# Gate and up: S3·T3 of four units in seven products, with kept parts read back by SyncE's queue

## The chip, the cores and the metric

The kernel runs on one core of a Trainium2 chip, in one launch. The metric is the device time of one execution in microseconds (us); a version's time is the median of its runs. The engines of a core run side by side, each through its own list of instructions, and wait for each other by semaphores: PE (TensorE, matmuls out of SBUF into the accumulators of PSUM), DVE (VectorE), ACT (ScalarE), POOL (GpSimd) and SP (SyncE, which here only starts DMAs). DMAs are started from SP, ACT and POOL; those that add onto their destination are started from POOL.

## The reference

All numbers are fp32; x is 2 x 2048 x 512. What is computed:

```python
x = x + attn(layernorm(x), Wq, Wk, Wv, Wo)      # softmax over 512 x 512 scores, per batch
n = layernorm(x)
gate = einsum('bsh,oh->bso', n, lut[gate_idx])  # 1376 rows; lut has 16 entries
up   = einsum('bsh,oh->bso', n, lut[up_idx])
out  = x + einsum('bsh,oh->bso', silu(gate) * up, lut[down_idx])
```

The change lies in `gate` and `up` and the product `silu(gate) * up`. The attention in front and the product with `down_idx` behind are the same in both kernels but for one choice of accumulators.

## The kernel before

**The stages.** By the clock of the profiled execution: Gram products of the normalised input to 78 us, squares and products of the attention's matrices to 180, the attention's output (y) to 286, gate and up to 748, the last 96 rows of gate and up to 789, the product down to the end.

**Gate and up.** The 1376 hidden rows are eleven blocks f of 128 (the last has 96), the 4096 tokens eight chunks of 512, taken in pairs p = 0..3. A unit (f, p) computes gate and up of block f for the two chunks of pair p. Eight units with f = 0 and 1 come first, then 32 units (f, p), f = 2..9, p = 0..3, in order; the eleventh block goes through `LastRows`. Block rows "gate, up" and the two halves of the contracted 512 make a 2 x 2 block matrix A, the two chunks and the two halves another, B. One level of Strassen's method in Winograd's form computes their product with seven block products instead of eight, with sums S1..S4 of A's blocks and T1..T4 of B's:

- a1 `11·11` gives p1; a2 adds `S2·T2` onto it in the same accumulator, giving u2; a3 adds `S1·T1`; a4 adds `S4·22`;
- c1 `S3·T3` gives p7; c2 adds `22·T4`;
- b adds `12·21` onto p1 and makes h0, the gate of the first chunk.

From these come h0 = silu(p1 + 12·21), times u2 + c; and h1 = silu(a after a4), times c22 = (a after a3) + p7. Each of the seven is two matmul calls of 128 x 512 (one per 128 rows of the contracted 256). A call is two matmul instructions in the profile, at line 1065 (`mm`).

**The second level.** Three of the seven products are themselves done for four units at once, by `Second` (line 946): `of_b` does `12·21`, `of_c` does `22·T4`, `of_d` does `S4·22`. The four units are two blocks f (even and odd) by two pairs p. The two calls of each unit are again a 2 x 2 product of blocks, eight calls, done as seven. Their left factors (of the weights) are summed per pair of f by `sums_left` (four sums on DVE), their right factors (of the tokens) once per group g = p // 2 by `sums`, in f = 1 and 2. These right factors T1, T2, T4 are written to DRAM (`far`) and read back when needed by `load`, on ACT's DMA queue, into tiles of tag "tt" (TT of them).

**Roles.** With f > 1 a unit has role 2·(f mod 2) + p mod 2: role 0 is the even f's first unit of the group, 1 its second, 2 the odd f's first, 3 its second. Role 1 also computes two products that belong to roles 2 and 3. They are copied out of PSUM by ACT (`part`, tiles of tag "rt", RT of them) and kept in DRAM as r6 (for role 2) and r5 (for role 3). Role 2 computes one more product and adds it onto r5 there, by POOL (`onto`). Roles 2 and 3 get their kept part back: `add_part` adds it onto p1 (of_b) and u2 (of_c) by a DMA of POOL, and `back` loads it as a tile y (of_d), also by POOL. With this, p=0 and p=1 are group 0, p=2 and p=3 group 1.

**Order.** The order of instructions on PE, ACT, DVE and SP is written out by hand in `Line.run`. The unit before (`last`) is finished within the unit that runs: its `first` (the product for h0 and its store, on SP), its `a4`, `end` (silu of h1) and `out` (the product for h1 and its store). At each `between` one due load, one entry of `todo`, and as many sums and steps of the weights' lookup as keep DVE within a lead (`leads[0]`, in us) of PE by a count of their costs are put in. The lookup makes the weights of later blocks from their indices on DVE (TENSOR_SCALAR at line 330, COPY_PREDICATED at line 342); after it come the four sums of a block (line 379). The helper `add` on DVE is line 172, `evict`, a copy on ACT, line 181; h1 and h0 are stored by SP at line 1092. DVE, ACT and PE each work through their list in order, so an instruction that waits holds all that stands behind it on its engine; the same is true of the DMA issues on SP and POOL.

**Accumulators.** PSUM has eight banks of 128 x 512: tag "a" has two, "c" two, and "b", "x", "z", "w" (of_b, of_c, of_d) one each. `Down` uses "a", "b" and "c".

Of the kernel before, what the change touches and what calls it, by code (L numbers as in the profile page):

```python
# [62 lines left out]
P = 128  # L63
# [6 lines left out]
def tile_attn_ffn(  # L70
# [874 lines left out]
    def psum(tag, name):  # L945
        return fps.tile([P, E], F32, tag=tag, name=name, bufs=2 if tag in "ac" else 1)

    class Second:
# [8 lines left out]
        def sums(self, g):  # L957
# [4 lines left out]
            def made(tag, u, v):  # L962
                r[tag] = x2p.tile([P, CH], F32, tag="tt", name=f"{tag}_{self.name}{g}", bufs=TT)
                sub(r[tag], u(), v())
                far = self.far[g, tag] = dram.tile(
                    [P, CH], F32, tag=f"{self.name}{g}{tag}", name=f"far_{self.name}{g}{tag}"
                )
                nc.gpsimd.dma_start(far, r[tag])
# [12 lines left out]
        def ready(self, f):  # L981
            return f in gu if self is of_d else f in uw
# [45 lines left out]
        def back(self, u):  # L1028

            t = u.temp("y")  # L1030
            nc.gpsimd.dma_start(t, self.parts[u.p // 2, {2: "r6", 3: "r5"}[u.role]])
            return t

    RT, TT = 3, 8
# [7 lines left out]
    seconds = [of_c, of_b, of_d]  # L1042
# [6 lines left out]
    def loads(f, p):  # L1049

        g = p // 2
        if 1 < f < NFT - 1 and f % 2 == 0 and p % 2:
            order = [(of_c, "T2"), (of_c, "T1")]
            order += [(o, tag) for tag in ("T2", "T1") for o in (of_d, of_b)]
        elif 1 < f < NFT - 1 and f % 2 and p % 2 == 0:
            order = [(o, "T4") for o in seconds]
        else:
            order = []
        return [lambda o=o, tag=tag: o.load(g, tag) for o, tag in order]
# [11 lines left out]
    class GateUp:  # L1071
# [32 lines left out]
        def extra0(self):  # L1104
            if self.role == 1:
                of_c.go_on(self, "S2", "T2")
                of_c.part(self, "r6")
            elif self.role == 2:
                of_c.begin(self, "S3", "T3")
                of_c.part(self, "r5", onto=True)  # L1110

        def c1(self):
            self.c = self.view("c")
            mm(self.c, self.pairs("S3", "T3"), True)
            self.p7 = self.temp("p7")
            evict(self.p7, self.c)
# [7 lines left out]
        def c2(self):  # L1124
            if self.role is None:
                mm(self.c, self.pairs("22", "T4"), False)
                add(self.u2, self.c, self.u2)
            elif self.role == 0:
# [3 lines left out]
                add(self.u2, self.c, self.u2)  # L1132
            elif self.role == 1:
                add(self.u2, self.c, self.u2)
                of_c.go_on(self, "S4", "22")
                add(self.u2, of_c.ps, self.u2)
            elif self.role == 2:
                of_c.go_on(self, "22", "T4")

        def extra1(self):  # L1140
            if self.role == 1:
                of_c.go_on(self, "S1", "T1")
                of_c.part(self, "r5")
            elif self.role == 2:
                of_b.begin(self, "S3", "T3")
                of_b.part(self, "r5", onto=True)

        def extra2(self):
            if self.role == 1:
                of_d.go_on(self, "S2", "T2")  # L1150
                of_d.part(self, "r6")
                of_b.go_on(self, "S2", "T2")
                of_b.part(self, "r6")

        def extra3(self):
            if self.role == 1:
                of_d.go_on(self, "S1", "T1")
                of_d.part(self, "r5")
                of_b.go_on(self, "S1", "T1")
                of_b.part(self, "r5")  # L1160
            elif self.role == 2:
                of_d.begin(self, "S3", "T3")
                of_d.part(self, "r5", onto=True)
            if self.role in (2, 3):
                self.y = of_d.back(self)

        def b(self):
# [14 lines left out]
            if self.role != 1:  # L1182
                nc.scalar.activation(h0, self.p1 if self.role in (None, 3) else h0, AF.Silu)

        def silu(self):

            if self.role == 1:
                nc.scalar.activation(self.h0, self.h0, AF.Silu)

        def a3(self):  # L1190
            mm(self.a, self.pairs("S1", "T1"), False)
            self.c22 = self.temp("c22")
            add(self.c22, self.a, self.p7)

        def first(self):
            if self.role == 2:
                add(self.u2, of_c.ps, self.u2)
            if self.role in (2, 3):
                add(self.u2, self.c, self.u2)
# [3 lines left out]
        def kept(self):  # L1203
            add(self.y, of_d.ps, self.y)

        def a4(self):
            self.h1 = h1 = self.temp("h1")
# [11 lines left out]
            else:  # L1219
                if self.role == 2:  # L1220
                    mm(self.a, of_d.pair(self, "22", "T4"), False)
                add(h1, self.a, self.y)
# [10 lines left out]
    class Line:  # L1233
# [5 lines left out]
        def run(self, u, final=False):  # L1239
            last, self.last = self.last, u  # L1240

            role = getattr(u, "role", None)
            u.a1()
            if last is not None:
                last.silu()
            self.between()
            before = getattr(last, "role", None)
            if before == 1:
                last.first()
            u.extra0()  # L1250
            u.c1()
            self.between()
            if before == 2:
                last.kept()
            elif before == 3:
                last.first()
            u.extra1()
            if role != 3 and last is not None:
                last.a4()
                self.between()  # L1260
            u.a2()
            if role == 3:
                self.between(0.0)
                last.a4()
                last.first()
                self.between(0.0)
            else:
                self.between()
            u.extra2()
            u.c2()  # L1270
            if last is not None:
                last.end()
            self.between()
            u.extra3()
            if last is not None:
                last.out()
            one, two = (u.a3, u.b) if final or role in (1, 3) else (u.b, u.a3)
            one()
            self.between()
# [3 lines left out]
            self.between()  # L1283
# [10 lines left out]
    class LastRows:  # L1294
# [17 lines left out]
        def weights(self):  # L1312
            w, v = self.w, self.v
            self.u = u = last_pool.tile([P, KB, 2 * LAST], F32, tag="last", name="last_2")
# [7 lines left out]
                lambda: minus(u[:, 3, :], v[:, 0, :], -1.0),  # L1322
            ]

        def pairs(self, c):

            w, v, u, x = self.w, self.v, self.u, xs[c // 2]
            second = c // 2 % 2
            if c % 2 == 0:
                one, two = (("11", w[:, 0:2, :]), ("21", w[:, 2:4, :], u[:, 0, :], u[:, 1, :]))  # L1330
            else:
                one, two = (("T3", v[:, 2:4, :]), ("22", v[:, 0:2, :], u[:, 2, :], u[:, 3, :]))
            t = x[one[0]]
            out = [(t[:, kk, :], one[1][:, kk, :]) for kk in range(2)]
            t = x[two[0]]
            if second:
                return out + [(t[:, 1, :], two[2]), (t[:, 0, :], two[3])]
            return out + [(t[:, kk, :], two[1][:, kk, :]) for kk in range(2)]
# [35 lines left out]
    leads = [1.4]  # L1374
# [102 lines left out]
    class Down:  # L1477
# [36 lines left out]
        def view(self, tag):  # L1514
            return psum(tag, f"{tag}_d_{self.name}")[:, :H]
# [61 lines left out]
        extra0 = extra1 = extra2 = extra3 = silu = end = out = first  # L1577
# [34 lines left out]
    for (f, p), following in zip(units, units[1:] + [(NFT, 0)]):  # L1612
# [11 lines left out]
        to_load[:] = loads(*following)  # L1624
# [141 lines left out]
```

## Time and profile before

| | us |
|---|---|
| median of 3 runs (1063.45 to 1063.8) | 1063.77 |
| the profiled execution | 1064.37 |
| its span, first to last instruction | 1062.6 |
| PE busy 12 to 78, of 66.00 | 65.94 |
| PE busy 78 to 180, of 102.00 | 101.69 |
| PE busy 180 to 286.3, of 106.30 | 106.30 |
| PE busy 286.3 to 391, of 104.70 | 104.70 |
| PE busy 391 to 747.7, of 356.70 | 356.70 |
| DVE busy 391 to 747.7 | 289.79 |
| PE busy 792 to 1062.6, of 270.60 | 266.93 |

The span is the time that the trace covers; the run's own time has 1.8 us more around it. The granted clock of TensorE is 1.00 throughout. PE counts as busy while a matmul runs, and small gaps of under a tenth of a us at the joints of instructions don't show in the sums of a stretch. In lines of the timeline the columns are start, duration, engine, line, operation, output<-input, shape, count; a bracket at the end tells the idle time before the instruction and what ended it. DMA lines give a queue, a count, KB each and the median time from issue to landing. Names in the profile: `a_g`, `c_g`, `b_g` are the accumulators of tags a, c, b in gate and up, `x_g`, `z_g`, `w_g` those of of_b, of_c, of_d; `hd` is the store of h0 and h1; `part_r_b`, `part_r_c`, `part_r_d` are the kept parts; `far_` the right factors in DRAM and `T_..._in` their loads; `ld`, `lc`, `lb` the sums of left factors.

### The profile page before, as it was taken

What the parts mean: (1) busy time and instruction counts of PE and PEld (TensorE: products, weight loads), DVE (VectorE), ACT (ScalarE), POOL (GpSimd) and SP (SyncE); (2) the same over time, 40 slices, a digit from 0 to 9 for tenths busy, and PEclk for the clock granted to TensorE, in tenths of its full rate; (3) what the DMA queues carried; (4) which work ended last, traced back from release to release, by engine and by line L of the source; (5) the groups of instructions that cost most, each with busy time, mean ns of one, the idle gap of its engine ahead of it and who ended that gap; (6) DMA issues with size and microseconds to landing.
All of it is one profiled execution on the core that took longest, in us unless ns stands there. A gap on an engine that the chain in (4) does not pass through costs nothing.

```text
span 1062.6 us, 11343 instructions
## 1 busy us (share of the span) xinstructions
PE 1055.5 (99%) x3554; PEld 661.3 (62%) x3554; DVE 803.3 (76%) x1538; ACT 385.1 (36%) x725; POOL 108.6 (10%) x160
## 2 busy tenths in 40 slices
PE   8999999999999999999999999999999999999998
PEld 5668887444444444444444444444998888888887
DVE  7888788898998897887988868849756455656554
ACT  4652532455542224444443444444222222211111
POOL 0000000012120120230141023014000000000000
PEclk9999999999999999999999999999999999999999
DMA  8650314589571366696697679569747665666773
GB/s 342 224 186 21 74 25 119 137 225 250 153 217 41 133 232 197 166 201 209 198 188 215 199 170 222 190 205 195 238 149 244 204 211 187 194 195 203 226 227 117
DMA packets 129084, 194.69 MB, mean 183 GB/s; under 512 B 18992, under 2 KB 59184, under 8 KB 127872
## 3 DMA queue, kind: packets, MB, share of 16 engines
q1 hardware_dynamic: 75904, 105.81, 31.4%
q0 software_dynamic: 15776, 39.92, 17.9%
q10 hardware_dynamic: 37344, 48.24, 14.0%
q8 instruction: 28, 0.46, 0.2%
q14 instruction: 32, 0.26, 0.1%
HBM read 111.42 MB, written 82.51 MB: 183 GB/s over the span
## 4 chain that ended last, share of the span: by engine, by line
PE 97%; DVE 1%; ACT 1%; DMA 0%; issue 0%; SPq 0%; ACTq 0%
PE a_g L1065 22%; PE a_d L1065 14%; PE y L839 10%; PE c_g L1065 8%; PE c_d L1065 7%; PE gp L522 6%; PE rows L1349 4%; PE b_d L1065 4%; PE x_g L1065 4%; PE z_g L1065 4%; PE w_g L1065 3%; PE b_g L1065 2%; PE ea_t L675 1%; PE ea_p L675 1%; PE ea_m L675 1%; PE ea_s L675 1%
## 5 line engine op out<-in xcount | busy, mean ns | idle before, releaser
L839 PE MATMUL y<-m,nT 128*128 128x512 f32 x256 | 110.2, 592 | 0.0
L342 DVE COPY_PREDICATED w<-b_w,w 128x1024 f32<-128x1024 int16 (+1 forms) x77 | 98.6, 1280 | 1.4
L839 PEld LDWEIGHTS y<-m,nT 128*128 128x128 f32 x256 | 48.5, 190 | 60.5 <-issue 57.3
L1065 PE MATMUL a_g<-xT_a,s 128*128 128x512 f32 x160 | 75.5, 594 | 0.0
L1065 PE MATMUL a_g<-xb,w 128*128 128x512 f32 x160 | 75.3, 593 | 0.0
L1065 PE MATMUL c_g<-xb,w 128*128 128x512 f32 x160 | 75.2, 592 | 0.0
L1065 PE MATMUL a_d<-dT,hs_a 128*128 128x256 f32 x288 | 72.6, 379 | 0.0
L522 PE MATMUL gp<-xn_a 128*128 128x128 f32 (+3 forms) x256 | 69.9, 434 | 1.7 <-DVE xn_a L223 1.7
L330 DVE TENSOR_SCALAR w<-idx_w,lut_x,lut_sb 128x1024 int32<-128x1024 int32 (+1 forms) x88 | 67.7, 794 | 0.2
L522 PEld LDWEIGHTS gp<-xn_a 128*128 128x128 f32 x256 | 43.9, 190 | 28.4 <-issue 15.1
L172 DVE TENSOR_TENSOR r<-r,p_d 128x256 f32<-128x256 f32 x64 | 27.1, 424 | 44.4 <-ACT p_d L181 41.5
L1065 PEld LDWEIGHTS a_d<-dT,hs_a 128*128 128x128 f32 x288 | 54.5, 189 | 7.7
L1065 PE MATMUL a_g<-xT_sq,s 128*128 128x512 f32 x120 | 56.7, 595 | 0.0
L181 ACT COPY p_d<-a_d 128x256 f32<-128x256 f32 x32 | 11.9, 372 | 121.4 <-PE a_d L1065 121.4
L1065 PEld LDWEIGHTS a_g<-xT_a,s 128*128 128x128 f32 x160 | 30.1, 190 | 38.9 <-issue 36.4
L1065 PEld LDWEIGHTS a_g<-xb,w 128*128 128x128 f32 x160 | 30.3, 190 | 38.5 <-issue 35.9
L1065 PEld LDWEIGHTS c_g<-xb,w 128*128 128x128 f32 x160 | 30.4, 190 | 38.3 <-issue 37.3
L342 DVE COPY_PREDICATED wd<-b_wd,wd 128x1024 f32<-128x1024 int16 (+1 forms) x42 | 50.7, 1208 | 0.8
L172 DVE TENSOR_TENSOR r<-r,a_d 128x256 f32<-128x256 f32 x64 | 26.8, 419 | 29.5 <-PE a_d L1065 29.5
L181 ACT COPY u<-a_g 128x512 f32<-128x512 f32 x40 | 23.4, 586 | 59.9 <-PE a_g L1065 57.3
L172 DVE TENSOR_TENSOR c<-a_g,p 128x512 f32<-128x512 f32 x40 | 27.6, 691 | 20.4 <-PE a_g L1065 19.0
L1349 PEld LDWEIGHTS rows<-last,xb 128*128 128x128 f32 x256 | 41.7, 190 | 0.5 <-issue 0.5
(357 smaller groups left out, 2086.2 us busy)
## 6 DMA issues: line engine op xcount, KB each, us to landing
hd<-h SPq DMA_DIRECT2D x80, 256.0 KB, 3.3
h<-hd SPq DMA_DIRECT2D x40, 512.0 KB, 6.3
nl<-nd SPq DMA_DIRECT2D x32, 256.0 KB, 5.8
xnd<-xn_f ACTq DMA_DIRECT2D x16, 512.0 KB, 4.6
fl<-xnd POOLq DMA_DIRECT2D x32, 256.0 KB, 6.1
xn_back<-xnd SPq DMA_DIRECT2D x32, 256.0 KB, 4.0
rd<-r SPq DMA_DIRECT2D x32, 256.0 KB, 3.2
r<-rd SPq DMA_DIRECT2D x32, 256.0 KB, 4.5
```

Of the source, the lines that this page charges most:

```text
L172: nc.vector.tensor_tensor(dest, a, b, op)
L181: nc.scalar.copy(dest, a)
L330: vec.tensor_scalar(dest.bitcast(I32), idx, lut_x[:rows, k : k + 1], lut_i[:rows, at : at + 1], ALU.bitwise_and, ALU.bitwise_xor,)
L342: vec.copy_predicated(dest, masks[level - 1], t)
L522: nc.tensor.matmul(gp[b][i][:, i * P :], xn[:, i, j % 2, :], xn[:, i:, j % 2, :], start=c % CPB == 0 and j == 0, stop=c % CPB == CPB - 1 a ...
L675: nc.tensor.matmul(ps[:, m, :], self.a[a][:, k, m * P : (m + 1) * P], self.b[b][:, k, :], start=first and m == k == 0, stop=k == 1, skip_g ...
L839: nc.tensor.matmul(ys[k], nTs[k][:, i, :], m[:, i, :], start=(i == 0), stop=(i == KB - 1))
L1065: nc.tensor.matmul(ps, lhsT, rhs, start=first and i == 0, stop=i == len(pairs) - 1, skip_group_check=not first,)
L1349: nc.tensor.matmul(ps[:, jj, :], x[:, j * P : (j + 1) * P], w, start=i == 0, stop=i == len(pairs) - 1,)
```

## The change

A fourth `Second`, `of_e`, does `S3·T3` for the four units. In PSUM tag "c" keeps one bank and a new tag "e" takes the other. Its parts of role 1 (r6, r5) are kept in DRAM as the others; role 2 adds its product onto r5. Roles 2 and 3 load their kept part of `of_e` as p7 (one buffer) and that of `of_d` straight into h1 (two buffers), both from SP's queue; the tile y goes. Role 2 adds its own `22·T4` of `of_e` onto p7 and adds p7 to u2 in `a3`; in role 3 p7 is added to u2 in `first`, within the next unit. The silu of h0 in role 3 moves to the start of the next unit's list. Role 0 computes `of_e`'s `11·11` in the new bank, copies it into c by ACT (`c0`) and adds `12·21` there (`c1`).

`run` now writes the order of each role out, in place of the stages `extra0` to `extra3`. Right factors of f = 1 are made in tiles of tag "rt" (RT 4 for 3), and "tt" has 6 tiles for 8; two of the eight loads of an odd p in an even f are issued in that unit itself (`late`). `leads` starts at 1.7 for 1.4. Since T3 of an odd pair is now changed in place too, `LastRows` takes a sum t of its weights for it; its tile `last_2` comes from another pool, and its sums are put into `todo` after the line is flushed. `Down` takes "c" and "e" in turn for its two halves.

```diff
     def psum(tag, name):
-        return fps.tile([P, E], F32, tag=tag, name=name, bufs=2 if tag in "ac" else 1)
+        return fps.tile([P, E], F32, tag=tag, name=name, bufs=2 if tag == "a" else 1)
...
             def made(tag, u, v):
-                r[tag] = x2p.tile([P, CH], F32, tag="tt", name=f"{tag}_{self.name}{g}", bufs=TT)
+                r[tag] = x2p.tile([P, CH], F32, tag="rt", name=f"{tag}_{self.name}{g}", bufs=RT)
...
-        def back(self, u):
-
-            t = u.temp("y")
-            nc.gpsimd.dma_start(t, self.parts[u.p // 2, {2: "r6", 3: "r5"}[u.role]])
+        def back(self, u, tag):
+            t = u.temp(tag, 2 if tag == "h1" else 1)
+            nc.sync.dma_start(t, self.parts[u.p // 2, {2: "r6", 3: "r5"}[u.role]])
             return t
 
-    RT, TT = 3, 8
...
-    seconds = [of_c, of_b, of_d]
+    of_e = Second("e", "e", lambda f: in_two(gu[f]["S3"]), lambda p: in_two(xs[p]["T3"]))
+    seconds = [of_c, of_b, of_d, of_e]
...
-    def loads(f, p):
+    def loads(f, p, late=False):
 
         g = p // 2
+        order = []
         if 1 < f < NFT - 1 and f % 2 == 0 and p % 2:
-            order = [(of_c, "T2"), (of_c, "T1")]
-            order += [(o, tag) for tag in ("T2", "T1") for o in (of_d, of_b)]
-        elif 1 < f < NFT - 1 and f % 2 and p % 2 == 0:
-            order = [(o, "T4") for o in seconds]
-        else:
-            order = []
+            order = [(o, tag) for tag in ("T2", "T1") for o in (of_c, of_e)]
+            order += [(of_d, "T2"), (of_b, "T2"), (of_d, "T1"), (of_b, "T1")]
+            order = order[TT:] if late else order[:TT]
+        elif 1 < f < NFT - 1 and f % 2 and p % 2 == 0 and not late:
+            order = [(o, "T4") for o in (of_e, of_b, of_c, of_d)]
         return [lambda o=o, tag=tag: o.load(g, tag) for o, tag in order]
...
         def c1(self):
-            self.c = self.view("c")
-            mm(self.c, self.pairs("S3", "T3"), True)
+            if self.role is None:
+                self.c = self.view("c")
+                mm(self.c, self.pairs("S3", "T3"), True)
+            else:
+                mm(self.c, of_e.pair(self, "12", "21"), False)
             self.p7 = self.temp("p7")
             evict(self.p7, self.c)
...
         def c2(self):
             if self.role is None:
                 mm(self.c, self.pairs("22", "T4"), False)
-                add(self.u2, self.c, self.u2)
-            elif self.role == 0:
+            else:
                 of_c.begin(self, "11", "11")
                 mm(self.c, of_c.pair(self, "12", "21"), False)
                 add(self.u2, of_c.ps, self.u2)
-                add(self.u2, self.c, self.u2)
...
+            add(self.u2, self.c, self.u2)
+
+        def c0(self):
+            of_e.begin(self, "11", "11")
+            self.c = self.view("c")
+            evict(self.c, of_e.ps)
+
+        def kept(self, o, a, b, tag, onto=False):
+            (o.begin if onto else o.go_on)(self, a, b)
+            o.part(self, tag, onto)
+
+        def c4(self):
+            of_c.go_on(self, "S4", "22")
+            add(self.u2, of_c.ps, self.u2)
+
+        def e4(self):
+            of_e.go_on(self, "S4", "22")
+            self.p7 = self.temp("p7")
+            evict(self.p7, of_e.ps)
+            add(self.u2, of_e.ps, self.u2)
+
+        def e3(self):
+            of_e.go_on(self, "22", "T4")
+            add(self.p7, of_e.ps, self.p7)
+
+        def c3(self):
+            of_c.go_on(self, "22", "T4")
+
+        def y_kept(self):
+            add(self.h1, of_d.ps, self.h1)
...
-            if self.role != 1:
-                nc.scalar.activation(h0, self.p1 if self.role in (None, 3) else h0, AF.Silu)
+            if self.role in (None, 0, 2):
+                nc.scalar.activation(h0, h0 if self.role is not None else self.p1, AF.Silu)
...
         def silu(self):
 
-            if self.role == 1:
-                nc.scalar.activation(self.h0, self.h0, AF.Silu)
+            if self.role in (1, 3):
+                nc.scalar.activation(self.h0, self.h0 if self.role == 1 else self.p1, AF.Silu)
...
         def a3(self):
             mm(self.a, self.pairs("S1", "T1"), False)
             self.c22 = self.temp("c22")
             add(self.c22, self.a, self.p7)
+            if self.role == 2:
+                add(self.u2, self.p7, self.u2)
 
         def first(self):
             if self.role == 2:
                 add(self.u2, of_c.ps, self.u2)
-            if self.role in (2, 3):
-                add(self.u2, self.c, self.u2)
+            elif self.role == 3:
+                add(self.u2, self.p7, self.u2)
             tensor(self.h0, self.h0, self.u2, ALU.mult)
             self.store(self.h0, 2 * self.p)
...
         def a4(self):
-            self.h1 = h1 = self.temp("h1")
+            if self.role not in (2, 3):
+                self.h1 = self.temp("h1", 2)
+            h1 = self.h1
...
-                add(h1, self.a, self.y)
+                add(h1, self.a, h1)
...
         def run(self, u, final=False):
             last, self.last = self.last, u
-
-            role = getattr(u, "role", None)
+            role, before = getattr(u, "role", None), getattr(last, "role", None)
+            go = self.between
+
+            def of_last(*stages):
+                for stage in stages if last is not None else ():
+                    getattr(last, stage)()
+
+            of_last("silu")
             u.a1()
-            if last is not None:
-                last.silu()
-            self.between()
...
+            if role == 3:
+                u.p7 = of_e.back(u, "p7")
+                last.c3()
+                last.y_kept()
+                go(0.0)
+                u.a2()
+                go(0.0)
+                of_last("a4", "first")
+                go(0.0)
+                u.h1 = of_d.back(u, "h1")
+                last.end()
+                go()
+                last.out()
+                u.a3()
+                go()
+                u.b()
+                go()
+                return
+            go()
...
+            if role == 1:
+                u.kept(of_c, "S2", "T2", "r6")
+                go()
+                u.kept(of_e, "S2", "T2", "r6")
+            elif role == 2:
+                u.p7 = of_e.back(u, "p7")
+                u.kept(of_c, "S3", "T3", "r5", True)
+                go()
+                u.kept(of_e, "S3", "T3", "r5", True)
+                u.kept(of_b, "S3", "T3", "r5", True)
+            else:
+                u.c1() if role is None else u.c0()
+                go()
+            if last is not None:
+                last.a4()
+                go()
+            if role == 1:
+                u.kept(of_c, "S1", "T1", "r5")
+            u.a2()
+            go()
+            if before == 3:
                 last.first()
-            u.extra1()
-            if role != 3 and last is not None:
-                last.a4()
-                self.between()
-            u.a2()
-            if role == 3:
-                self.between(0.0)
-                last.a4()
-                last.first()
...
+            if role == 1:
+                u.kept(of_e, "S1", "T1", "r5")
+                u.kept(of_d, "S2", "T2", "r6")
+                u.kept(of_b, "S2", "T2", "r6")
+                u.c4()
+            elif role == 2:
+                u.kept(of_d, "S3", "T3", "r5", True)
+                u.h1 = of_d.back(u, "h1")
+                u.e3()
             else:
-                self.between()
-            u.extra2()
-            u.c2()
...
+            of_last("end")
+            go()
+            if role == 1:
+                u.e4()
+                u.kept(of_d, "S1", "T1", "r5")
+                u.kept(of_b, "S1", "T1", "r5")
+            of_last("out")
+            one, two = (u.a3, u.b) if final or role == 1 else (u.b, u.a3)
...
-            self.u = u = last_pool.tile([P, KB, 2 * LAST], F32, tag="last", name="last_2")
+            u = wgu.tile([P, 3, 2, P], F32, tag="s", name="last_2", bufs=3)
+            u = self.u = u.rearrange("p a b c -> p (a b c)").rearrange("p (k r) -> p k r", k=KB)
+            self.t = t = last_pool.tile([P, 2 * LAST], F32, tag="last", name="last_3")
...
+                lambda: add(t, v[:, 2, :], v[:, 3, :]),
...
-    leads = [1.4]
+    leads = [1.7]
...
-            return psum(tag, f"{tag}_d_{self.name}")[:, :H]
+            return psum("ce"[self.jj] if tag == "c" else tag, f"{tag}_d_{self.name}")[:, :H]
...
-        to_load[:] = loads(*following)
+        to_load[:] = loads(f, p, late=True) + loads(*following)
...
+                todo += by_two(last_rows.weights() + down_sums(0, hps["dT"]))
```

Left out of the diff are the old stages that `run` no longer calls (`extra0` to `extra3`, `kept`) and the lines of `LastRows.pairs` that choose between the two forms of its factors.

## The prediction

> **What bounds the kernel now.** I read the busy times first, then the chain of waits, then the stretches of gate and up, then its timeline, then the DMA issues. All of the first say TensorE (PE).
>
> ```profile
> PE 1055.5 (99%) x3554; PEld 661.3 (62%) x3554; DVE 803.3 (76%) x1538; ACT 385.1 (36%) x725; POOL 108.6 (10%) x160
> ...
> PE 97%; DVE 1%; ACT 1%; DMA 0%; issue 0%; SPq 0%; ACTq 0%
> ...
> L1065 PE MATMUL c_g<-xb,w 128*128 128x512 f32 x160 | 75.2, 592 | 0.0
> ```
>
> The chain is PE for 97%, so a product removed is time removed, as long as nothing that feeds PE comes later than today. The next lines are two stretches of gate and up, the first with an even f, the second with an odd f (us, then busy time and instructions of PE, PEld, DVE, ACT, POOL, granted clock, share of the DMA engines, GB/s):
>
> ```profile
> 394.00:432.00 38.00, 38.00 (x90) 16.91 (x89) 30.51 (x47) 17.23 (x30) 1.62 (x3) 1.00 0.57 187
> 434.00:475.00 41.00, 41.00 (x97) 17.95 (x96) 35.12 (x59) 17.44 (x29) 15.91 (x19) 1.00 0.87 183
> ```
>
> PE has no idle time in either; the clock is full. The odd stretch is the tight one: DVE is 86% busy there and the DMA engines 87%, POOL issues 19 instructions. The timeline of the end of one unit and the start of the next shows what PE, DVE and SyncE (SP) do:
>
> ```profile
> 564.16 0.68 DVE L172 TENSOR_TENSOR u<-z_g,u 128x512 f32<-128x512 f32 x1
> 564.88 0.69 DVE L172 TENSOR_TENSOR u<-c_g,u 128x512 f32<-128x512 f32 x1
> 565.15 1.88 PE L1065 MATMUL a_g<-xb,w 128*128 128x512 f32 x4
> 565.67 0.69 DVE L172 TENSOR_TENSOR h<-h,u 128x512 f32<-128x512 f32 x1
> 566.28 0.69 DVE L172 TENSOR_TENSOR h<-h,c 128x512 f32<-128x512 f32 x1
> 566.39 0.92 SPq L1092 DMA_DIRECT2D hd<-h  x2
> 566.87 1.88 PE L1065 MATMUL c_g<-xb,w 128*128 128x512 f32 x4
> ```
>
> From it: 4 matmul instructions start to start take 1.72 us, so a product of 128x512 (one call, two instructions) takes 0.86 us (0.8575 over longer runs); a DVE add takes 0.69, 0.61 start to start where it depends on nothing just before it; SP issues the store as the product h<-h,u ends. The second issue waits for h<-h,c (end 566.97) and the row ends at 567.31: 0.33 us an issue.
>
> **What it removes.** S3·T3 of four units is seven products for eight. 32 units make eight groups, so 8 calls go, 16 matmul instructions: 8 x 0.8575 = **-6.86 us**, all on PE.
>
> **What it adds off the path.** Per group: three loads of T1, T2, T4 of the new factor and two stores of kept parts on ACT's queue, one more accumulate by POOL, two loads of p7 by SP; the two loads of y move from POOL to SP, as h1. ACT makes two copies more (0.59 us each) and DVE one add, plus four sums of 0.23 us per pair of f: 2.3 us per pair, which is 79 us long and has 13 us of idle DVE time. The six differences and two in-place ones in f=1 and 2 (about 5.5 us of DVE) fall where DVE has 9.8 us idle (94.87 busy of 104.7 us from 286.3 to 391). These I cost at nothing; without that slack the four pairs would show 9 us. The T loads are asked for 9 to 12 us ahead and landed in at most 5.0; the kept parts have 3.9 us until their buffer is wanted (such stores landed in 2.0 to 2.5 us in the even stretches, in one of them in 4.0 for r_b, so this is the nearest to the edge). POOL's odd-stretch queue gets shorter (two accumulates more, four loads fewer, in 19). The last rows get one more sum of their weights and Down takes its two banks as c and e in turn instead of c twice: the order is the same, cost nothing. The larger lead (1.7 for 1.4) lets DVE's lookups go ahead of PE a little further; the same idle time hides it.
>
> **One product between copy and use.** PE must wait where an accumulator is copied to SBUF and added to again with one product between. The timeline shows such a place (the copy u<-a_g, then the last two calls of the unit):
>
> ```profile
> 471.35 1.02 PE L1065 MATMUL a_g<-T_d_in,s 128*128 128x512 f32 x2
> 471.55 0.59 ACT L181 COPY u<-a_g 128x512 f32<-128x512 f32 x1 [1.09 <-PE a_g L1065]
> 472.20 1.96 PE L1065 MATMUL a_g<-xT_sq,s 128*128 128x512 f32 x4
> 474.00 1.88 PE L1065 MATMUL a_g<-xb,w 128*128 128x512 f32 x4
> ```
>
> 472.20 to 474.00 is 1.80 where 1.72 is four matmuls: 0.09 lost. In the order after, this form is new at a2 behind the copy of p1 (p=1 of odd f: 4), at a2 behind b_g (p=0 of f=4, 6, 8: 3) and at c's second half behind p7 (p=2 of even f: 4; p=0 of f=2: 1): 12 x 0.09 = **+1.1 us**; at most twice that, at least 0.
>
> **First new wait: SP's two loads in a row (unit p=3 of each odd f).** I count from the start of unit (odd f, 2). PE has 15 products until a2 of unit (f, 3), which so stands at 12.86 us. It needs the copy of p1 to be done; ahead of that copy on ACT stands the silu of h0, which needs the DVE sum h0 = x + p1, which stands on DVE behind p7 += e, which waits for the load of p7. That load is issued by SP only when DVE has read the old p7 (one buffer) in u2 += p7, and this stands on DVE behind h1 += a, which waits for the load of the *other* kept part, h1, which stands on SP behind the store of h0. With L for one such load: the store goes out at 0.5 (before, h<-h,u ended 1.21 us after the unit's start, and the add u<-c_g, 0.7, is no longer ahead of it), the load of h1 at 0.85, landing at 0.85 + L. DVE has other work until 3.96 (a product, c22, two COPY_PREDICATED of 1.16). Then h1 += a 0.61, four sums 1.47, u2 += p7 0.69; issue 0.03; L; three adds 1.91; silu 0.68; copy 0.6. That is 6.85 + 2L, or 9.96 + L for L below 3.1: against 12.86 a stall of **2L - 6.01**, at L below 3.1 of L - 2.9. Behind the waiting add on DVE stand the sums and lookups; what PE then lacks is counted in the stall, and everything later moves with it. Four such units (f=3, 5, 7, 9).
>
> **Second new wait (unit p=0 of f=4, 6, 8).** The multiply-add of role 3 is now finished in the next unit. c's second half needs the copy of the new p7, which waits for u2 += p7 of the unit before; this stands on DVE behind h1 += a, behind the load of h1, at 0.85 + L from the unit's start. DVE itself is free at 3.95 (product, c22, eight sums for the left sides, a mask). Then 0.61, two masks 0.8, 0.69, copy 0.64. PE stands there at 6.09. Stall **L - 2.5**, not under 0.6. Three times.
>
> **L.** Loads of 256 KB by SP in an odd stretch do not exist before. These rows of 434 to 475 us are the nearest:
>
> ```profile
> q0 software_dynamic: 2238, 4.55, 67.4%
> q1 hardware_dynamic: 1008, 1.84, 12.1%
> ...
> hd<-h SPq DMA_DIRECT2D x6, 256.0 KB, 4.0
> ...
> T_c_in<-far_c1T ACTq DMA_DIRECT2D x1, 256.0 KB, 4.6
> T_b_in<-far_b1T ACTq DMA_DIRECT2D x1, 256.0 KB, 5.0
> T_d_in<-far_d1T ACTq DMA_DIRECT2D x1, 256.0 KB, 3.8
> ```
>
> The same T loads took 2.7, 2.7, 4.0; 3.1, 4.9, 3.7; 2.9, 5.0, 3.9 in the other three odd stretches; the twelve have a mean of 3.86, and I take that; the ends are 2.7 and 5.0. The load on the engines rises: POOL's 17.4 transfers take 67.4% of 41 us, 1.59 each; the hardware queue's seven 12.1%, 0.71 each. Ten more of the second and two fewer of the first are +7.1 - 3.2 = 3.9 us, 0.87 to 0.97 of the engines. The Trainium skill, "DMA: Bandwidth & Descriptors", section "Issuing engines are not separate DMA queues", says that transfers started from any engine run on the same 16 DMA engines and that another issuer saves only its issue time; it speaks against any gain from SP's queue beyond POOL's 0.57 us an issue. The trace agrees: SP's own stores took 2.0 us in the even stretch and 4.0 in the odd one, where the other queue fills the engines. The same page, "Anatomy of one DMA", gives 2.0 us plus bytes/436e3 per DMA for POOL's path; for 256 KB my estimate from it is 2.6 us, and the sum would then be -4.0 us (1059.8) where the rows give +5.1; the rows decide.
>
> **Sum.** -6.86 + 1.08 + 4(2L - 6.01) + 3(L - 2.5) = 11L - 37.3. At L = 3.86: +6.84 and +4.08 of stalls, **+5.1 us**. The profiled run has 1064.37 (span 1062.6), 0.6 above the median of 1063.77; I put the difference on the median: **1068.9 us**.
>
> **Rivals.**
> (A) The loads are quick (L up to 3.2) and the waits lie beside PE's work: -6.86 + 1.08, four stalls of at most 0.4 and three of 0.6 to 0.7: 1060 to 1061.6; with no stall at all 1058. For it: even-stretch landings of 2.0 to 2.7. Against: the share of 0.87 and the dependence on two landings in a row. It is faster; it decides below L = 3.2.
> (B) L between 3.2 and 3.59: the stalls eat the saving, within 2.1 us of before, about 1064. For it: the T loads' spread straddles it.
> (C) the forecast, L from 3.59 to 4.6: 1066 to 1077.
> (D) Engines at 0.97 push L over 4.6, and p1's accumulate (landing 4.0 to 5.8 before, 5.5 us of room) holds the silu of role 3 too: from L = 4.6 the sum is over 13.3 us, above 1077.
>
> **How the numbers follow.** 0.2% of 1063.77 is 2.1 us, about what a measurement of this kernel can tell from no change. A 0.23, B 0.17, C 0.52, D 0.08: faster 0.23, same 0.17, slower 0.60. The time is that of C at L = 3.86. The range takes in A's quick loads and C's end: 1060 to 1077; C's own is 1066 to 1077.
>
> **What would show it.** PE's idle time before a2 behind p1's copy, in p=3 of f=3, 5, 7, 9: 1.7 us each. Idle before c's second half in p=0 of f=4, 6, 8: 1.4 each. DVE idle before h1 += a and p7 += e, released by SP's loads landing in about 3.9 us. 16 matmuls fewer. I am wrong if those loads land in 3 us, if PE's busy share in the odd stretches stays at 100%, or if PE waits for T loads or for POOL's accumulates instead.

## The result, and the profile after

The changed kernel takes 1112.51 us (median of 4 runs, 1110.1 to 1112.75) against 1063.78 (4 runs): 1.0453 times as long, 95% interval 1.0435 to 1.0472. The prediction was slower, 1068.9 with a range of 1060 to 1077; the direction was right, the size was not. The profiled execution took 1112.75 us. Its page, the busy times, the granted clock by fortieths of the span and the chain of waits:

```profile
span 1111.0 us, 11474 instructions
...
PE 1064.4 (96%) x3538; PEld 660.9 (59%) x3538; DVE 815.6 (73%) x1571; ACT 390.3 (35%) x741; POOL 107.8 (10%) x158
...
PEclk9999999999999999989989998999899999999999
...
PE 29%; DMA 1%; DVE 0%; ACT 0%; issue 0%; DVEq 0%
```

The chain, followed back from the end, breaks off in this kernel after some 30% of the span, so it says nothing of gate and up. PE executes 16 instructions fewer, as it should, and yet is busy 8.9 us longer; the clock, full before, has dents in slices 18, 21, 25 and 29. What PE waited for:

```profile
PE a_g L1065 <- ACT p L181: 32.1, 7, 7.8
PE a_g L1065 <- DVE h L172: 4.6, 2, 3.9
PE c_g L1065 <- ACT p L181: 3.3, 4, 1.3
...
PE e_g L1065 <- DVE le L172: 0.4, 1, 0.4
```

The columns are us in total, times, the longest. Before, none of these rows was there. The same two kinds of stretch as before, an even f and the odd f behind it (now 48.2 us long for 41):

```profile
396.00:434.00 38.00, 38.00 (x89) 16.76 (x90) 29.46 (x47) 18.92 (x33) 2.85 (x6) 1.00 0.74 250
437.30:485.50 48.20, 38.47 (x83) 16.32 (x82) 31.16 (x51) 15.21 (x27) 15.59 (x18) 0.89 0.84 199
```

The even one is still full of PE. The odd one has nearly 10 us without PE, and a mean clock of 0.89. This is the place, in the timeline from the start of unit (3, 2) on:

```profile
457.76 1.88 PE L1065 MATMUL a_g<-xb,w 128*128 128x512 f32 x4
...
459.16 0.45 SPq L1030 DMA_DIRECT2D h<-part_r_d  x1
...
466.51 0.69 DVE L172 TENSOR_TENSOR h<-a_g,h 128x512 f32<-128x512 f32 x1 [3.44 <-DMA h<-part_r_d]
...
468.58 0.68 DVE L172 TENSOR_TENSOR u<-p,u 128x512 f32<-128x512 f32 x1
469.29 0.32 SPq L1030 DMA_DIRECT2D p<-part_r_e  x1
469.78 1.02 PE L1065 MATMUL z_g<-T_c_in,w 128*128 128x512 f32 x2
...
475.37 0.69 DVE L172 TENSOR_TENSOR p<-e_g,p 128x512 f32<-128x512 f32 x1 [5.32 <-DMA p<-part_r_e]
...
477.29 0.63 ACT L1173 ACTIVATE h<-h 128x512 f32<-128x512 f32 x1 [9.43 <-DVE h L172]
477.83 0.57 ACT L181 COPY p<-a_g 128x512 f32<-128x512 f32 x1
478.45 3.78 PE L1065 MATMUL a_g<-xT_x,s 128*128 128x512 f32 x4 [7.65 <-ACT p L181]
```

Read from the bottom: PE stood 7.65 us for the copy of p1, this behind the silu of h0, this behind DVE, which sat 5.32 us until the load of p7 landed; that load went out only when u2 += p7 had read the old p7, which came late because DVE had sat 3.44 us for the load of h1. The two loads took 7.35 us (459.16 to 466.51) and 6.08 us (469.29 to 475.37), from issue to the start of the add that waited. Not every unit is like this one. Over all of gate and up DVE waited for loads and accumulates of kept parts so (us in total, times, the longest):

```profile
DVE p L172 <- DMA p<-part_r_e: 29.9, 7, 6.9
...
DVE u L172 <- DMA u<-part_r_c: 11.8, 4, 6.1
...
DVE h L172 <- DMA h<-part_r_d: 4.5, 4, 3.4
```

The load of p7 was waited for in every long pause; of the waits for h1, 3.44 us are the one shown. The row of u is POOL's accumulate of of_c's kept part onto u2.

In the place shown, four matmul instructions then took 3.78 us where four took 1.88 before. The reason stands in the table of stretches, whose third figure from the right is the granted clock (then the share of the DMA engines, then GB/s):

```profile
467.00:473.00 6.00, 3.80 (x9) 1.33 (x7) 2.92 (x7) 0.63 (x1) 0.13 (x1) 1.00 1.12 207
473.00:479.00 6.00, 0.55 (x1) 0.50 (x2) 3.63 (x7) 1.10 (x2) 0.31 (x1) 0.55 0.47 173
479.00:485.00 6.00, 6.00 (x9) 2.31 (x8) 2.88 (x11) 0.89 (x2) 1.43 (x2) 0.59 0.47 95
```

The clock fell to half during the pause and stayed there for some us into the work behind it.

**Where the 48.7 us are.** From start to start of the matmuls in gate and up I took what exceeds 0.4287 us an instruction. Before, it is 0.7 us (8 places of 0.09 to 0.10). After, it is 56.5 us. 56.5 - 0.7 - 6.86 (the products saved) = 48.9, the whole of the difference. It divides so:

| | us |
|---|---|
| a2 of (odd f, 3): 7.65, 6.54, 7.80, 6.64 | 28.6 |
| a2 of (odd f, 1): 2.08, 0.44, 0.93; a1 of (odd f, 2): 0.68, 3.92 | 8.0 |
| c's second half: 0.58, 1.00, 1.30 in p=0 of f=4, 6, 8; 0.39 once in p=2 | 3.3 |
| le in f=2 | 0.4 |
| the rest: matmuls at half clock, and 21 small pauses (2.2 in all) | 16.2 |

The last row agrees with the page: PE is busy 1064.4 us, where 1055.5 less 6.86 would be 1048.6, 15.8 more.

### The profile page after: what moved, and what is told of

It reads as the page before. It is cut to its first block, busy times and chain, and to the rows that moved or that the text cites. A ratio compares the mean times of both kernels' runs of the same rounds, so it can differ in the third digit from the quotient of the medians.

```text
span 1111.0 us, 11474 instructions
## 1 busy us (share of the span) xinstructions
PE 1064.4 (96%) x3538; PEld 660.9 (59%) x3538; DVE 815.6 (73%) x1571; ACT 390.3 (35%) x741; POOL 107.8 (10%) x158
## 3 DMA queue, kind: packets, MB, share of 16 engines
q0 software_dynamic: 16128, 39.40, 16.2%
q10 hardware_dynamic: 43104, 58.73, 16.2%
## 5 line engine op out<-in xcount | busy, mean ns | idle before, releaser
L1065 PE MATMUL a_g<-xT_x,s 128*128 128x512 f32 x40 | 26.4, 796 | 28.6 <-ACT p L181 28.6
L172 DVE TENSOR_TENSOR h<-a_g,h 128x512 f32<-128x512 f32 x32 | 22.0, 687 | 41.7 <-ACT h L181 24.7
L172 DVE TENSOR_TENSOR r<-r,a_d 128x256 f32<-128x256 f32 x64 | 26.8, 418 | 27.4 <-PE a_d L1065 27.2
L1382 PE MATMUL rows<-last,xb 128*128 128x192 f32 x256 | 41.8, 326 | 0.0
```

The costliest lines, as they stand in the source:

```text
L172: nc.vector.tensor_tensor(dest, a, b, op)
L1065: nc.tensor.matmul(ps, lhsT, rhs, start=first and i == 0, stop=i == len(pairs) - 1, skip_group_check=not first,)
L1382: nc.tensor.matmul(ps[:, jj, :], x[:, j * P : (j + 1) * P], w, start=i == 0, stop=i == len(pairs) - 1,)
```

## The experiments

Three theories stood against each other first. (1) One buffer for p7 puts two landings in a row, these are long because the DMA engines are over-full, and the long pauses lower the clock. (2) The place of the loads on SP, behind the stores. (3) DVE late by its own sums and lookups. Where only one time is given, it was one run, beside runs of the kernel before of 1063.76 to 1063.9 (one, or the median of seven); the changed kernel's own four runs lie 2.65 us apart.

**Two buffers for p7.**

```diff
-    RT, TT = 4, 6
+    RT, TT = 4, 5
-            t = u.temp(tag, 2 if tag == "h1" else 1)
+            t = u.temp(tag, 2)
-            self.p7 = self.temp("p7")
+            self.p7 = self.temp("p7", 2)
```

> p7 gets a second buffer (room for it: 5 tiles of tag tt for 6). Theory 1, one buffer for p7 makes SP's load of p7 in unit (odd f, 2) wait for u2 += p7, which waits for the load of h1, so two landings of 5 to 6 us stand in a row before a2 of (odd f, 3), and the long pauses then lower PE's clock: the four pauses of 6.5 to 7.8 us fall to under 1.5 us, the ones before c's second half (0.6 to 1.3) vanish, PE's busy time falls from 1064.4 to about 1049, and the time to 1060 to 1070. Theory 2, the place of the loads on SP's queue behind the stores of h0 and h1 holds them: the buffer changes little, time 1100 to 1113. Theory 3, DVE runs late by its own sums and lookups: no change, 1108 to 1113.

Measured: 1086.42 us (4 runs, 1085.23 to 1090.86), ratio to before 1.0208 (1.0191 to 1.0225).

```profile
PE a_g L1065 <- ACT p L181: 13.0, 7, 3.6
PE a_g L1065 <- DVE h L172: 7.6, 4, 2.5
...
PE c_g L1065 <- ACT p L181: 0.4, 1, 0.4
```

The pauses before c's second half vanished but for one, the four long ones became 3.62, 0.45, 0.46 and 1.76; so the one buffer is a cause, worth up to 26 us of 49 (the next run tells what the sixth tile has in that). The waits shown are those of the slowest of the four runs. It is not the whole: 1086 is far from the 1060 to 1070 expected. In (3, 2) the load of h1 now landed 9.4 us after its issue (459.70 to 469.06), and that of p7 12.1 us (461.14 to 473.19). The order is mended; the landings are longer still.

**The control: five tiles for six.** Only the line of RT and TT.

> The control for p7two: 5 tiles of tag tt for 6 and nothing else, so one more load of a right factor is asked for only in the unit that uses it. All theories: within 2 us of the changed kernel's 1112.5; if that load comes late, PE would pause before the first product of of_b in role 1 and the time be up to 8 us longer.

1108.17 us, 4.3 less than the changed kernel, where at most 2 were expected. The missing tile accounts for at most some 4 of the 26 us; 22 are left for the buffer. Why one tile fewer is no slower was not tried.

**The order on SP.**

```diff
                 go(0.0)
+                u.h1 = of_d.back(u, "h1")
                 of_last("a4", "first")
                 go(0.0)
-                u.h1 = of_d.back(u, "h1")
```

> In role 3 the load of h1 is put on SP ahead of the store of h0 of the unit before instead of behind it. Theory 1: it is issued some 1.3 us earlier at best, or held by the landing of the accumulate onto r5 of of_d; the two landings stay in a row, so eight chains of roles 2 and 3 get 0 to 1.3 us shorter, and the time is 1100 to 1113. Theory 2 (order on SP): the pauses go, time under 1080. Theory 3: no change.

1104.29 us: as theory 1 has it, 8 us and not 30.

**The loads back on POOL.** In `back`, `nc.gpsimd.dma_start` for `nc.sync.dma_start`.

> The loads of p7 and h1 go back to POOL's queue, the rest as changed. Theory 1: they stand behind the accumulates' issues of 0.6 to 0.9 us each, their landings stay at 5 us or more, and the two in a row stay: 1105 to 1125. Theory 2 (SP's queue is the cause): the pauses go, 1060 to 1075. Theory 3: no change, 1112.

1117.88 us, the longest pause 10.97 us. The queue that issues the loads is not the cause; with POOL's the run was even 5.4 us longer. Theory 2 falls with these two.

**Without the accumulates onto r5.**

```diff
             if onto:
-                nc.gpsimd.dma_start(self.parts[g, tag], t, accum_op=ALU.add)
                 return
```

The output then lacks role 2's products.

> Left out: role 2's own S3 T3 products are computed and copied but not added onto r5 (8 of the 18 accumulating transfers of an odd f); the rest is the changed kernel. Theory 1b, the DMA engines are over-full in the units of role 2, where six accumulates of some 1.6 us of all 16 engines each meet the loads of p7, h1 and four T4 in 10.3 us: SP's loads land in 3 to 4 us for 5 to 6.4, the pauses before a2 of (odd f, 3) fall below 2 us, the clock stays at 1.00, and the time is 1060 to 1072. Rival, SP's loads are slow by themselves: landings stay at 5 us or more and the time over 1095.

1086.36 us. The DMA issues of the stretch from 440 to 478 us, first of the changed kernel, then of this one:

```profile
p<-part_r_e SPq DMA_DIRECT2D x3, 256.0 KB, 6.0
h<-part_r_d SPq DMA_DIRECT2D x3, 256.0 KB, 6.4
u<-part_r_c POOLq DMA_DIRECT2D x3, 256.0 KB, 8.9
part_r_c<-r_c POOLq DMA_DIRECT2D x2, 256.0 KB, 6.8
part_r_e<-r_e POOLq DMA_DIRECT2D x2, 256.0 KB, 7.8
part_r_b<-r_b POOLq DMA_DIRECT2D x2, 256.0 KB, 9.3
part_r_d<-r_d POOLq DMA_DIRECT2D x2, 256.0 KB, 9.0
```

```profile
p<-part_r_e SPq DMA_DIRECT2D x4, 256.0 KB, 2.8
u<-part_r_c POOLq DMA_DIRECT2D x4, 256.0 KB, 4.2
h<-part_r_d SPq DMA_DIRECT2D x3, 256.0 KB, 3.9
```

The landings fall as expected (and the accumulates that are left land in 4.2 for 8.9), and with them the share of the DMA engines: from 441 us on, by 10 us, it was 0.93, 1.03 and 1.08 in the changed kernel and is 0.63, 0.82 and 0.79 here. Another way in which the accumulates could act is by order, since the loads of role 3 read what was accumulated. In the changed kernel this held none of SP's: those loads of h1 went out 2.9 us or more, those of p7 3.3 us or more, after the accumulate they need had landed. So it is the engines' load that makes the landings long, and the accumulates are a large part of it. But the time was expected at 1060 to 1072.

```profile
PE a_g L1064 <- ACT p L181: 15.0, 4, 4.6
```

The four pauses were still 4.64, 2.90, 3.05 and 4.41: at the place that counts, in (3, 2), the load of h1 took 8.15 us (456.69 to 464.84), behind four T loads and two loads of indices issued 2 to 6 us before it; p7's took 2.74. A median over a stretch hides this place.

**Without of_e's accumulate alone.**

> Left out: only the accumulate of of_e's product onto its r5, the two of an odd f that the change adds. Theory 1b: some of the overload goes, landings of 4.5 to 6 us, time 1085 to 1105. Rival: no change, 1108 to 1113.

1103.85 us, 8.7 us less, at the upper end: the two transfers of an odd f that the change adds are not all. The other six, which the kernel before had too, are the rest of the 26.2 us, 17.5.

**Both.**

> Both: two buffers for p7, and (left out) role 2's products not added onto r5. Theory 1 with both halves: nothing is left of the long pauses, PE idles under 4 us in gate and up, and the time is 1057 to 1062, so that the saving of 6.86 us less the one-product gaps shows. If it stays above 1066, a third cause is open.

1065.49 us, clock 1.00 throughout. The output again lacks role 2's products. The two causes together are 47 of the 48.7 us. What is left of the pauses:

```profile
PE a_g L1064 <- ACT p L181: 4.5, 4, 2.0
...
PE e_g L1064 <- DVE le L172: 0.4, 1, 0.4
PE c_g L1064 <- ACT p L181: 0.4, 1, 0.4
```

By the start-to-start count 9.2 us are lost in gate and up here, 2.9 of them in 31 pauses of 0.07 to 0.15 us behind a copy with one product between; 9.2 - 0.7 - 6.86 is +1.6, as measured (+1.7). So there was a third part, and 1057 to 1062 was too low: four pauses behind the copy of p1 (0.36 to 2.05 us) and the small ones are most of it.

**And the load of h1 earlier, with both.**

> Left out: role 2's products are not added onto r5. Two buffers for p7, and the load of h1 ahead of the store of h0. What was left in p7two_noacc (1065.5) were six pauses of 0.4 to 2.1 us before a2 behind p1's copy and 31 small ones of 0.07 to 0.11. Theory 1: the landing of h1 behind that store is the rest of it, 1 to 2 us in each odd f go, time 1059 to 1063.5: the saving of 6.86 us then shows less the small pauses. Otherwise 1065 to 1067.

1064.29 us, between the two outcomes: 1.2 less, with 8.3 us still lost (2.7 of them small). The saving of 6.86 us is eaten even where the DMA engines have room; this version, which leaves products out, is level with the kernel before.

**Work in the pause.**

```diff
+                if u.p == NPR - 1:
+                    spare = u.view("c")
+                    lhsT, rhs = u.pairs("11", "11")[0]
+                    for _ in range(8):
+                        nc.tensor.matmul(spare, lhsT, rhs, start=True, stop=True)
                 u.a2()
```

> Eight products into the accumulator c, which nobody reads then, stand on PE before a2 of each unit (odd f, 3): 4 x 6.9 us of work in place of pauses of 6.5 to 7.8 us. If it is the pause that lowers PE's clock, the clock stays at 1.00 there, the first two products behind it take 1.9 us for 3.8, and the time falls by 8 to 16 us to 1096 to 1105 in spite of more work. Rival, PE is slow there because its operands or the memories are busy with transfers: unchanged, 1109 to 1116.

1103.95 us, with 27.4 us more matmuls on PE than the changed kernel:

```profile
471.86 1.02 PE L1065 MATMUL z_g<-T_c_in,w 128*128 128x512 f32 x2
472.72 7.03 PE L1250 MATMUL c_g<-xb,w 128*128 128x512 f32 x16
479.58 1.88 PE L1065 MATMUL a_g<-xT_x,s 128*128 128x512 f32 x4
```

The four instructions behind take 1.88 us again, at full clock. PE's busy time, 1082.3, less the 27.4 and less 1048.6 leaves 6.3 of the 15.8 us: it is the pause that lowers the clock, and the 9.5 us between are about the 8.6 by which the run is shorter than the changed kernel.

**Two buffers for p7, and h1 early.**

> Two buffers for p7, and the load of h1 in role 3 ahead of the store of h0 on SP. With the chain of two landings gone, the load of h1 (issued at 0.85 us of the unit, landing 6 to 9 us later) is what holds DVE in p7two. Theory 1: 1 to 2 us taken from each of the seven or so places where PE waits for DVE's h, time 1074 to 1084 (p7two 1086.4). If the accumulate onto r5 of of_d, which lands 8 to 10 us after its issue, holds the earlier issue: no gain, 1085 to 1090.

1086.38 us: no gain over p7two, the second of the two outcomes. What held the earlier load is in the landings of this run. In two of the eight units of role 3 it went out 0.02 us after of_d's accumulate had landed; in the other six it went out 0.05 to 0.08 us after a store of h had landed, and the accumulate had landed 0.7 to 2.5 us before. So the cause that was expected holds for two; in six a store's landing came last, the accumulate's shortly before it.

**A complete kernel without those accumulates.** First of_d's and of_e's: of_d's product is added to h1 of role 3 from its accumulator, of_e's copy in SBUF to p7.

```diff
+            if onto and self is of_d:
+                return
...
+            if onto and self is of_e:
+                self.t = t
+                return
...
+                else:
+                    add(h1, of_d.ps, h1)
                 add(h1, self.a, h1)
...
+                add(u.p7, of_e.t, u.p7)
                 u.a3()
```

> p7 with two buffers, and role 2's own products of of_d and of_e reach role 3 without the DMA: of_d's is added to h1 on DVE out of its accumulator, of_e's copy in SBUF is added to p7 on DVE; 4 of the 18 accumulates of an odd f go, DVE gets two adds of 0.69 us a group more. Theory 1b (over-full DMA engines): SP's loads land in 4 to 5 us, time 1068 to 1080 (p7two 1086.4, p7two_noacc 1065.5). If DVE is the limit there instead: over 1086.

> As direct_de, but of_b's and of_c's copies are added too, on POOL (to p1 and u2 before the accumulate of the kept part); no accumulate onto r5 is left and the output is the same. Theory 1b: as p7two_noacc, 1063 to 1070; the add on POOL delays p1's accumulate by 1 to 2 us, which may cost up to 1.5 us in each of the eight units of role 3.

1102.94 and 1104.42 us: both missed. In direct_all the loads of p7 and h1 land in 3.8 and 4.5 us in the median (singly 2.6 to 9.0); but PE waits elsewhere:

```profile
PE w_g L1069 <- DVE h L172: 6.0, 4, 3.4
PE a_d L1069 <- DVE r L172: 5.4, 2, 4.2
PE x_g L1069 <- ACT r_b L1016: 4.8, 3, 3.5
PE z_g L1069 <- DVE lc L172: 4.3, 1, 4.3
PE e_g L1069 <- DVE le L172: 3.9, 3, 2.7
```

lc and le, the left sums, come late (and in Down, DVE's r): my reading is that lookups were put off, since the planner adds DVE's new sums to its count, and puts in less of the lookups at each step. Three more, all with the load of h1 early, the last two with `leads` at 2.5 and 3.5 besides:

> direct_all with the load of h1 ahead of the store of h0 on SP. Nothing holds the earlier issue here, since no accumulate onto r5 is left: 1 to 4 us less than direct_all, 1060 to 1067.

> direct_all_h1early (1089.8) with DVE's lead at 2.5 us for 1.7. There PE waited some 19 us for lookups that had been put off (lc, le, the rows' and Down's weights) and for r_b's copies. If the order on DVE is what is left, more lead brings the lookups forward: 1068 to 1080. If DVE is simply full, 1085 to 1095.

> The same with a lead of 3.5 us: if more lead helps, 1062 to 1075; but each result that PE waits for is then up to 1 us later on DVE, and if that decides it is above the run with 2.5.

1089.79, 1073.84 and 1086.82 us. With a lead of 2.5 the waits for lookups are gone (of DVE's left sums only 0.4 us is left, of r nothing), so these waits came from their order, not from DVE's fullness; at 3.5 the time is longer again. 1073.84 is the best complete version with S3·T3 in seven products, 0.9% above the kernel before.

**The lead of before.** `leads = [1.4]` in the changed kernel.

> The changed kernel with the lead of DVE's lookups back at 1.4. Theory 1: DVE's own order has little part in the pauses, 1108 to 1116. Theory 3 (DVE is late by its own work): 1 to 2 us less at each of some ten waits, 1090 to 1104.

1136.7 us, on the far side of both. The long pauses stay (8.92, 5.03, 6.07, 8.70), and lookups come late too: PE waited 7.6 us for lc and le (and 9.0 once in Down behind a copy, whose cause is open). My reading, not shown, is that the planner's count knows nothing of the pauses, so that its lookups fall the further behind the longer they are. Theory 3 is wrong for the long pauses: with less lead two are longer and two shorter, 28.7 us in all for 28.6. But DVE's order is worth 24 us here, and more lead was not tried in the changed kernel itself.

## Why the prediction was wrong, by its steps

- **The saving, 6.86 us.** Right: 16 instructions fewer, and the sum of the losses closes only with it.
- **Off the path.** Right for PE: no product waited for a T load or an index. But their cost came back through the engines: T loads of 6.7 and 7.7 us stand in the same burst, where the prediction had at most 5.0.
- **One product between copy and use, 12 x 0.09 = 1.1.** Half the size: 31 of them in p7two_noacc, 2.9 us for 0.7 before, so 2.2, the upper bound that was given.
- **First new wait, 2L - 6.01.** Place and last half of the chain were right in all four units: the load of p7 was waited for. **The step that failed is L**: 3.86 was put in, and the eight loads of these four units took 5.2 to 7.7 us but for one of 3.0 (h1 in f=9). Four such pauses were priced at 6.8 us and took 28.6. With 2L taken as the two measured landings, 6.85 + 7.35 + 6.08 - 12.86 = 7.4 us against 7.65 in f=3; in f=5, with 5.48 and 6.50, 6.0 against 6.54; in f=7, with 5.17 and 7.67, 6.8 against 7.80. In f=9 the form fails too: 2.96 and 6.48 give 3.4 against 6.64. The first half, DVE waiting for h1, is seen in f=3 (3.44 us) and f=5 (0.41); in f=7 DVE came 0.4 us after that landing. In f=9 DVE was late by lookups, four rows of 5.7 us between 771.46 and 777.71, and the load of p7 went out only at 778.31.
- **Second new wait, L - 2.5.** Right in place and about in size: 0.6 to 1.3 in f=4, 6, 8, 2.9 us for 4.1; the loads there landed in 2.9 to 3.3.
- **Missed: waits one unit earlier.** p=1 and the start of p=2 of odd f lost 8.0 us, and the sum had no term for them. The 3.4 us before a2 of p=1 stand behind the load of p7. The 4.6 us before a1 of p=2, in f=7 and 9, stand behind POOL's accumulate onto u2, for which DVE sat 3.25 and 6.08 us: one of the signs of being wrong that the prediction named. In noacc none of these pauses is left.
- **Missed: the clock.** Pauses were priced as lost time alone. Some 14 us more (16.2 less 2.2 of small pauses) are matmuls at half clock. The sum 11L - 37.3 had no such term. Together: of the 43.6 us between forecast and result 21.8 are the four long pauses, 8.0 the waits one unit earlier and 14 the clock; the rest cancels to within 0.3.
- **Why L failed.** The share of the DMA engines was averaged over the 41 us of an odd stretch, 0.87, to which 0.10 was added. By 10 us the profile before already had

```profile
441.00:451.00 10.00, 10.00 (x24) 4.37 (x23) 8.72 (x13) 3.75 (x8) 4.69 (x6) 1.00 1.01 199
451.00:461.00 10.00, 10.00 (x24) 4.29 (x23) 7.77 (x14) 5.63 (x9) 3.87 (x4) 1.00 0.98 255
461.00:471.00 10.00, 10.00 (x25) 4.45 (x24) 9.52 (x22) 3.61 (x6) 4.11 (x5) 1.00 1.00 192
```

  a share of 1.01, 0.98 and 1.00 (the last figure but one) for 30 us, just where the new loads go. There was no room. The T loads taken for L were issued in that same stretch (449.15 to 452.58 in f=3) and landed in 3.8 to 5.0. The prediction's own window, 434 to 475 us, had a nearer row, which it left out: the loads of of_d's kept part, which the change moves to SP.

```profile
y<-part_r_d POOLq DMA_DIRECT2D x3, 256.0 KB, 5.1
```

  At L = 5.1 the sum 11L - 37.3 is +18.8, outside the range, and still far from +48.7. The first half of rival (D), with a chance of 0.08, was the case: L over 4.6. Its price "above 1077" had no upper end.

The Trainium skill, "TensorE: Matmul & The Clock Gate", section "HAM oscillation — how this bites in real kernels", says that a wait for data which crosses one of the clock gate's windows (about 3.4 us) throttles TensorE again, so that the work behind it starts at half rate. For the long waits these runs agree: every pause before a2 or a1 from 3.92 us up was followed by matmuls at half rate (four instructions in 3.5 to 3.8 us for 1.9). Shorter ones differ from it in part: 2.15, 2.50 and 2.86 us were followed by slow matmuls, and one of 1.97 in tt5 by four in 2.79 us; 2.45, 3.31 and 3.71 were not.

The same skill's "DMA: Bandwidth & Descriptors", section "Issuing engines are not separate DMA queues", says that transfers run on the same 16 DMA engines whichever engine started them. poolback agrees: with the loads on POOL's queue the four pauses stay, 7.0 to 11.0 us.

## What to carry to other kernels

Read the load of the DMA engines at the place where a new transfer lands, in stretches as short as the transfer's chain, not over a stage: at the four places of the long pauses, 19 to 20 us each, the share was 0.87 to 1.00, and all loads of p7 and h1 but one took 5.2 to 7.7 us where 3.86 was expected; with eight accumulates of an odd f left out the median for p7 fell from 6.0 to 2.8 in f=3. Take the price of a landing from transfers of the same tensor, where the profile has them. Where a buffer's reuse puts two landings in a row, the price is two landings under that load, and a second buffer takes one out. Price a TensorE pause of some 2 us or more with a half clock that may follow; from 3.92 us up it always did here.

## What was not expected of the hardware

The trace's clock shows half speed for 42 us of the changed kernel, in stretches of 3.4, 6.8 and 10.2 us (and 1.0 at its end), against 1.2 us at the end of the kernel before. In a unit of role 2 of p7two, where ten transfers of 256 KB were issued in 8 us (459.2 to 467.2), two plain loads took 9.4 and 12.1 us; one of the same size took 2.74 in noacc. A POOL add of 128x512 in SBUF took 1.26 to 1.74 us in direct_all, and one DVE sum of 0.29 us took 1.36 beside it (473.92); what that costs in all was not tried, but direct_de, without such adds, was only 1.5 us shorter.
